# Second layernorm's rows turned on VectorE in 32 by 32 blocks instead of on TensorE, and the adapters' first product taken from the last GEMM's own operands

## The chip, the cores and the metric

The kernel runs on one core of a Trainium2 chip, in one launch. The metric is the device time of a whole execution in microseconds (us). Five engines run side by side, each with its own queue of instructions in a fixed order: TensorE (PE in the profile, with its weight loads as PEld), VectorE (DVE), ScalarE (ACT), GpSimd (POOL), and SyncE (SP), which here does nothing but issue the transfers between DRAM and on-chip memory (SBUF). They meet through semaphores only.

## The reference, cut to what matters

Eight sequences of 512 rows with 1024 columns, all in float32, go through an attention layer and a feed-forward layer. Both layers are set between two layernorms without scale or shift:

```python
x = x + layernorm(attention(layernorm(x)))      # 16 heads of 64, rotary, causal
x = x + layernorm(ffn(layernorm(x)))

def ffn(x):                                     # x: (8, 512, 1024)
    y = x @ weight.T + bias                     # 1024 x 1024
    A, Bw = lora_A[adapter_of_batch], lora_B[adapter_of_batch]   # rank 16, three adapters
    return y + use_lora * ((x @ A.T) @ Bw.T)    # per batch
```

The part that the change touches lies between `layernorm(x)` of the second line and the two products that read it. Both contract over the 1024 columns. TensorE contracts over the partitions of SBUF (128 of them), so the normalised rows, which are made with a row in each partition, must be turned: columns to the partitions, rows to the free axis.

## The kernel before

**Passes and ticks.** The last stage of the kernel is a loop over 16 passes, `q` = 0 to 15 (`products`, called at the end). Pass `q` below 8 multiplies the attention output of batch `q` with the output projection; pass `q` of 8 and above multiplies the normalised rows of batch `q - 8` with the feed-forward weight. Each pass is a 512 x 1024 x 1024 product done by two nested Strassen-like schemes of seven products each. That makes 49 small products, and each is one *tick*: two matmuls of 128 x 128 (stationary) by 128 x 256 (moving). `Group` holds seven ticks, in the order `SLOTS`; the groups come in the order `ORDER`. The stationary operand is a slot of `RX[q, n]` (the row side: `R11`, `R21`, `R12`, `R22` and the sums `T1` to `T4`, each tile with seven slots of 2 x 128 values); the moving one is a slot of the weights.

**What sets the order.** The order is written out by hand: `at(tick, fn)` hangs work on a tick, and `run(tick, ...)` emits, for each tick, first the extra TensorE work (`"pe"`), then the tick's product and the draining of the tick before, then everything else. So all engines' queues are interleaved by tick, and a queue may run ahead or behind only as far as its semaphores allow. Pass `q` starts at tick `49 q`.

**The accumulators.** A group adds its products in PSUM tiles `a` (one buffer), `b` (two), `c` (two) and `d` (one). `drain` empties them: ScalarE copies `a`, VectorE does the additions from `b`, `c` and `d` (line 337). `combine` (line 355) adds whole quarters on VectorE and GpSimd.

**The rows.** `plan_rows(q, base)` hangs the layernorms of pass `q`'s result on ticks that reach into pass `q + 1`: for row tile `t` (128 rows, four per batch), `k = base + 55 + 7 t`. There are statistics on VectorE, the normalisation on ScalarE (line 415), the residual sum on GpSimd (`add_row`, line 1107), the store of the sum (line 1112), then, for `q` below 8, statistics and normalisation again. The normalised rows land in the tile `row`. At `k + 20` and `k + 21` (ticks 26, 27 of the next pass for tile 0, then 33, 34, then 40, 41, then 47, 48) `transpose_x1` turns half a row tile each: four TensorE transposes into a PSUM tile `ptf` (line 1121), which ScalarE copies to `xT` (`keep_x1`, line 1125). `xT` has one buffer, for two row tiles. When two row tiles are turned, `lora_in` (line 1131) multiplies them with the adapters' A (eight matmuls, 64 x 256 each), `lora_keep` (line 1139, VectorE) masks the result to the batch's adapter, and `store_x1` stores it (`ht`, line 1144) and the turned rows (`x1t`, line 1145) to DRAM.

**The reading back.** In the passes from 7 on, `plan_right` loads the next pass's `R11`, `R21`, `R12`, `R22` at ticks 10, 17, 24 and 31 (`load_right`, line 255: four slots of raw rows in one transfer), and four ticks later GpSimd makes the other three slots and overwrites slot 2 with a difference (`sub_right`, line 263, the four steps of `SUM_R`). The sums `T1` to `T4` follow (line 275). `load_ht` (line 1084) reads `ht` back at tick 3 of the pass that uses it, and `sub_ht` (lines 1088 and 1089, GpSimd) makes its differences one tick later; the adapters' second product (line 322) uses them from tick 11 on.

**The loads' releasers.** A load of `R..` can only be issued when the last product that read its buffer is done; in the trace SP waits for that product at each of the four loads. All transfers go through SP's one queue. In both programs' instruction lists each transfer also waits for the transfer eight places before it in that queue: eight semaphores are used in turn.

Of the kernel before, what the change touches and what calls it, by code (L numbers as in the profile page):

```python
# [10 lines left out]
F32 = mybir.dt.float32  # L11
I32 = mybir.dt.int32
AF = mybir.ActivationFunctionType
ALU = mybir.AluOpType
# [16 lines left out]
ALL = slice(None)  # L31
# [101 lines left out]
def sandwich_kernel(  # L133
# [15 lines left out]
    nc = tc.nc  # L149
# [16 lines left out]
    x1t = [dram.tile([P, NT, NK, P], F32, name=f"x1t_{b}") for b in range(B)]  # L166
    htd = [dram.tile([P, S], F32, name=f"ht_{b}") for b in range(B)]


    vd = [dram.tile([P, NT, E], F32, name=f"vd_{b}") for b in range(B)]  # L170
# [23 lines left out]
    def at(tick, fn, kind=None):  # L194
        events[tick].append((kind, fn) if kind else fn)
# [14 lines left out]
    RX = {}  # L210
    C = {}
    hts = {}
# [34 lines left out]
    def load_right(pool, q, n):  # L247

        g, h = int(n[1]) - 1, int(n[2]) - 1
        open_right(pool, q, n)  # L250
        if q < B:
            nc.sync.dma_start(out=RX[q, n], in_=attn[q][:, g, h])
            return
        src = x1t[q - B]
        nc.sync.dma_start(
            out=RX[q, n][:, 0:4].rearrange("p (t k) c n -> p t (k c n)", t=2),
            in_=src[:, 2 * h : 2 * h + 2, ts(g, NH), :].rearrange("p t k n -> p t (k n)"),
        )

    def sub_right(q, n, eng):  # L260
        t = RX[q, n]
        for out, x, y in SUM_R:
# [21 lines left out]
    def open_c(q, tag):  # L284
# [3 lines left out]
            [P, 2, HALF], F32, tag=tag, bufs=1 + two, name=f"{tag}_{q}"  # L288
        )

    class Group:


# [7 lines left out]
        def product(self, p):  # L301
            l, r, a = SUBS[p]
            first = a not in self.acc
            if first:
                self.acc[a] = env["acc"].tile(
                    [P, SUB], F32, tag=a, bufs=ACCS[a], name=f"acc{a}_{self.name}"
                )
            acc = self.acc[a]
            left, right = self.W[self.L], RX[self.q, self.R]
            for k in range(2):  # L310
                if self.q < 0:
                    moving = left[:, SLOT_L[l], k, :]
                else:
                    moving = left[:, 4 * k : 4 * k + 4, SLOT_L[l], :]
                nc.tensor.matmul(  # L315
                    acc, lhsT=right[:, SLOT_R[r], k, :], rhs=moving,
                    start=(first and k == 0), stop=True, skip_group_check=True,
                )
            if self.lora and p in LORA_SUB:
                half, cols = self.lora  # L320
                i, c = LORA_SUB[p]
                nc.tensor.matmul(  # L322
                    acc, lhsT=hts[self.q - B][:, cols[c], :],
                    rhs=env["lb"][:, half * HALF + i * SUB : half * HALF + (i + 1) * SUB],
                    start=False, stop=True, skip_group_check=True,
                )
# [210 lines left out]
    for b in range(B):  # L537
        base = b * N2
# [514 lines left out]
    with ExitStack() as a:  # L1053
# [22 lines left out]
        at(N2 + 30, load_adapters)  # L1076

        NQ = 2 * B
        hto = {}

        def load_ht(b):

            t = hts[b] = lc.tile([P, 9, P], F32, tag="htb", name=f"htb_{b}")
            nc.sync.dma_start(out=t[:, 0:4], in_=htd[b][:, :].rearrange("p (t n) -> p t n", t=NT))

        def sub_ht(b):
            t = hts[b]
            nc.gpsimd.tensor_tensor(t[:, 4:6], t[:, 0:2], t[:, 2:4], op=ALU.subtract)
            nc.gpsimd.tensor_tensor(t[:, 6:9], t[:, 0:6:2], t[:, 1:6:2], op=ALU.subtract)  # L1089
# [23 lines left out]

        xT = {}

        def transpose_x1(q, t, g):
            if (q, t // 2) not in xT:
                xT[q, t // 2] = cp.tile([P, 2, NK, P], F32, tag="xT", name=f"xT_{q}_{t // 2}")
            pt = ps_t.tile([P, NH, P], F32, tag="tp", name=f"ptf_{q}_{t}_{g}")
            for k in range(NH):  # L1120
                nc.tensor.transpose(pt[:, k, :], row[q, t][:, ts(NH * g + k, P)], ident)
            return pt

        def keep_x1(q, t, g, pt):
            nc.scalar.copy(xT[q, t // 2][:, t % 2, ts(g, NH), :], pt)

        def lora_in(q, h):
            ph = ps_t.tile([P, NH, P], F32, tag="tp", name=f"ph_{q}_{h}")
            for k in range(NK):
                r = (k % 2) * HD  # L1130
                nc.tensor.matmul(  # L1131
                    ph[r : r + HD, 0:2, :], lhsT=la_sb[:, k, :], rhs=xT[q, h][:, :, k, :],
                    start=(k < 2), stop=(k >= NK - 2),
                )
            return ph

        def lora_keep(q, h, ph):
            ht = hto[q, h] = lc.tile([P, 2 * P], F32, tag="ht", name=f"ht_{q}_{h}")
            nc.vector.tensor_scalar(
                ht, ph[:, 0:2, :], sel[:, q : q + 1], idx_sb[:, 1:2], op0=ALU.mult, op1=ALU.add  # L1140
            )

        def store_x1(q, h):
            nc.sync.dma_start(out=htd[q][:, h * 2 * P : (h + 1) * 2 * P], in_=hto[q, h])
            nc.sync.dma_start(out=x1t[q][:, 2 * h : 2 * h + 2], in_=xT[q, h])

        def plan_right(q, base):

            if q > 1:
                at(base + 6, next_roles)  # L1150
            for n, k in (("R11", 10), ("R21", 17), ("R12", 24), ("R22", 31)):
                if q == 1 and n != "R22":
                    continue
                at(base + k, lambda n=n: load_right(gp, q, n))
                if q >= B:
                    at(base + k + 4, lambda n=n: sub_right(q, n, nc.gpsimd))
            for n, k in (("T1", 40 if q == 1 else 38), ("T2", 45), ("T4", 52), ("T3", 63)):
# [14 lines left out]
        def plan_rows(q, base):  # L1172

            for t in range(NT):
                k = base + 55 + 7 * t
                key = f"{'o' if q < B else 'y'}{q}_{t}"
                at(k + 2, lambda t=t: load_row(q, t))
                for m in range(4):
                    at(k + m, lambda t=t, m=m, key=key: stats(key, halves(q, t), m))
                for h in range(2):  # L1180
                    at(k + 4 + h, lambda t=t, h=h, key=key: norm(key, halves(q, t)[h], halves(q, t)[h]))
                    at(k + 6 + h, lambda t=t, h=h: add_row(q, t, h))
                at(k + 12, lambda t=t: store_rows(q, t))
                if q < B:
                    key = f"x{q}_{t}"
                    for m in range(4):
                        at(k + 12 + m, lambda t=t, m=m, key=key: stats(key, halves(q, t), m))
                    for h in range(2):
                        at(k + 16 + h, lambda t=t, h=h, key=key: norm(
                            key, row[q, t][:, ts(h, HALF)], halves(q, t)[h]  # L1190
                        ))
                    for g in range(2):
                        at(k + 20 + g, lambda t=t, g=g: transpose_x1(q, t, g), "pe")
                        at(k + 20 + g, lambda pt, t=t, g=g: keep_x1(q, t, g, pt), "post")
                    if t % 2:
                        at(k + 23, lambda t=t: lora_in(q, t // 2), "pe")
                        at(k + 23, lambda ph, t=t: lora_keep(q, t // 2, ph), "post")
                        at(k + 26, lambda t=t: store_x1(q, t // 2))

        def plan_last(q, base):  # L1200

# [159 lines left out]
```

## Time and profile before

| | us |
|---|---|
| median of 3 runs | 2499.29 (2498.07 to 2499.87) |
| span of the profiled execution | 2491.9 |
| what the median has around that span | 7.4 |
| the stage with the 16 passes: pass 1 starts at | 1703.57 |
| pass 7, 8, 9, 10 start at | 2007.28, 2062.78, 2119.65, 2171.19 |
| pass 15 starts at | 2425.44 |

The profile is of one execution on the chip; its own time is known by its span, from the first to the last instruction. A pass's start is the start of its first product in the TensorE timeline. In the last 16 passes the profile is to be read pass by pass: the passes below 8, those from 9 on, and the two at the seam (7 and 8, in which the feed-forward weights are loaded) are bound differently. Durations are of single instructions; a matmul's duration is longer than its pace, since matmuls are pipelined, so a pace is read from the starts of neighbours.

### The profile page before, as it was taken

Reading aid. Unit: us, or ns where it says so; the run is one execution under the profiler, and the core shown is the slowest. Engines: PE = TensorE matmul, PEld = TensorE weight load, DVE = VectorE, ACT = ScalarE, POOL = GpSimd, SP = SyncE. Lnnn points to the kernel's source line nnn. Section 1 sums busy time; section 2 is a strip of 40 time slices with the busy share of each in tenths; the row PEclk is TensorE's granted clock in tenths of the full one; section 3 lists DMA queues with packets and bytes.
Section 4 is the critical chain, followed back from the end, with each engine's and each line's share of the span. In section 5 each row is a group of like instructions: output and inputs, shape, how many; then the busy total and the mean of one; then the engine's idle time right before and its main releaser. Section 6 shows DMA issues by size and latency. Waiting matters only on the chain. (4 is left out here: it accounts for less than half of the span.)

```text
span 2491.9 us, 37087 instructions
## 1 busy us (share of the span) xinstructions
PE 2394.2 (96%) x12192; PEld 1880.4 (75%) x12192; DVE 1744.9 (70%) x3849; ACT 1094.4 (44%) x2749; POOL 1490.5 (60%) x1119
## 2 busy tenths in 40 slices
PE   6999999999999999999999999899999999999997
PEld 4787887877677777777777776458888878888886
DVE  8777767475857759486775957766777777766676
ACT  3323331026555556555555565763444544222222
POOL 3878875215263454637465363426777687888885
PEclk8999999999999999999999999899999999999999
DMA  7697787999899898988989895657566676434334
GB/s 261 198 299 251 241 272 235 344 307 285 238 302 285 258 328 255 328 267 297 326 264 346 250 327 174 219 182 266 178 202 212 217 278 240 137 126 153 132 106 140
DMA packets 415665, 606.00 MB, mean 243 GB/s; under 512 B 127889, under 2 KB 243601, under 8 KB 410866
## 3 DMA queue, kind: packets, MB, share of 16 engines
q1 hardware_dynamic: 415474, 603.64, 73.9%
q8 instruction: 98, 1.61, 0.3%
q14 instruction: 93, 0.76, 0.1%
HBM read 368.65 MB, written 201.33 MB: 229 GB/s over the span
## 5 line engine op out<-in xcount | busy, mean ns | idle before, releaser
L778 ACT ACTIVATE pr<-pr,nm 128x128 f32<-128x128 f32 (+3 forms) x512 | 280.9, 550 | 169.7 <-DVE nm L768 169.6
L792 ACT ACTIVATE pr<-pr,rs 128x128 f32<-128x128 f32 (+2 forms) x500 | 245.2, 549 | 119.9 <-DVE rs L786 119.8
L768 DVE CUSTOM_DVE_ANT_0 pr<-s,mask 128x128 f32<-128x128 f32 (+3 forms) x512 | 224.1, 484 | 41.8 <-PE s L747 39.7
L636 PE MATMUL acca_q_P<-xs,ls 128*128 128x256 f32 x896 | 217.3, 385 | 0.8 <-issue 0.8
L636 PE MATMUL accc_q_P<-xs,ls 128*128 128x256 f32 x896 | 217.7, 386 | 0.0
L636 PE MATMUL accb_q_P<-xs,ls 128*128 128x256 f32 x896 | 216.3, 384 | 0.8 <-DVE u_q_P L116 0.8
L1107 POOL TENSOR_TENSOR c<-c,row 128x512 f32<-128x512 f32 x120 | 160.7, 1360 | 87.4 <-ACT c L415 80.3
L636 PEld LDWEIGHTS acca_q_P<-xs,ls 128*128 128x128 f32 x896 | 165.3, 190 | 49.9 <-issue 19.1
L636 PEld LDWEIGHTS accc_q_P<-xs,ls 128*128 128x128 f32 x896 | 165.8, 190 | 48.4 <-issue 23.2
L636 PEld LDWEIGHTS accb_q_P<-xs,ls 128*128 128x128 f32 x896 | 165.4, 190 | 44.9 <-issue 6.2
L275 POOL TENSOR_TENSOR T<-R,T 128x512 f32<-128x512 f32 (+1 forms) x96 | 174.1, 1840 | 41.4 <-DVE u_P L337 21.0
L747 PE MATMUL s<-qk 64*128 64x128 f32 (+3 forms) x1024 | 193.8, 474 | 5.1 <-DVE nm L768 4.7
L806 PE MATMUL ptp<-ident,pr 128*128 128x128 f32 x1280 | 178.7, 278 | 11.0 <-DVE nm L768 4.8
L806 PEld LDWEIGHTS ptp<-ident,pr 128*128 128x128 f32 x1280 | 147.7, 142 | 43.1 <-ACT pr L792 15.8
L827 PE MATMUL po<-pT,v 128*64 128x512 f32 (+3 forms) x1024 | 157.4, 446 | 9.7 <-ACT pT L821 9.7
L562 POOL TENSOR_TENSOR wc_g<-wc_g 128x256 f32<-128x256 f32 (+1 forms) x120 | 124.1, 1053 | 65.5 <-DMA wc_g<-in_wqk_dram 43.5
L678 POOL TENSOR_TENSOR B_q<-B_q,m 128x1024 f32<-128x1024 f32 x14 | 35.0, 2497 | 199.0 <-DVE B_q L675 199.0
L827 PEld LDWEIGHTS po<-pT,v 128*64 128x64 f32 x1024 | 72.4, 139 | 102.0 <-issue 66.5
L337 DVE TENSOR_TENSOR p_P<-accb_P,p_P 128x256 f32<-128x256 f32 x109 | 45.0, 413 | 102.4 <-PE accb_P L315 53.5
L636 PE MATMUL accd_q_P<-xs,ls 128*128 128x256 f32 x448 | 108.7, 385 | 0.0
L337 DVE TENSOR_TENSOR u_P<-accb_P,p_P 128x256 f32<-128x256 f32 x109 | 46.1, 423 | 89.1 <-ACT p_P L342 89.0
L747 PEld LDWEIGHTS s<-qk 64*128 64x128 f32 x1024 | 73.1, 187 | 46.2 <-issue 27.9
(1108 smaller groups left out, 5809.7 us busy)
## 6 DMA issues: line engine op xcount, KB each, us to landing
ls<-wqk SPq DMA_DIRECT2D x392, 256.0 KB, 4.9
xs<-xop SPq DMA_DIRECT2D x392, 256.0 KB, 5.2
R<-attn SPq DMA_DIRECT2D x32, 896.0 KB, 5.5
wqk<-wc_g SPq DMA_DIRECT2D x16, 1568.0 KB, 9.3
x<-in_x_dram SPq DMA_DIRECT2D x32, 512.0 KB, 9.5
v<-vd SPq DMA_DIRECT2D x64, 256.0 KB, 5.0
attn<-ops SPq DMA_DIRECT2D x16, 1024.0 KB, 7.8
row<-in_x_dram SPq DMA_DIRECT2D x32, 512.0 KB, 5.9
```

The source lines that it names most:

```text
L275: eng.tensor_tensor(RX[q, n][:, c], RX[q, x][:, c], RX[q, y][:, c], op=ALU.subtract)
L337: add = lambda out, x, a: nc.vector.tensor_tensor(out, acc[a], x, op=ALU.add)
L562: eng.tensor_tensor(out, x, y, op=op)
L636: nc.tensor.matmul(acc[:, :, w, :], lhsT=ls[:, k, w, :], rhs=xs_[:, :, k, :], start=(first and w == 0 and k == 0), stop=True, skip_group_c ...
L678: eng.tensor_tensor(v, v, m[step - 4, q], op=ALU.add)
L747: nc.tensor.matmul(ps[:, j, at : at + L], lhsT=qT[r, qb], rhs=kT[r, : qb + 1], start=True, stop=True,)
L768: nc.vector.tensor_tensor_reduce(out=v[:, j, :], in0=self.ps[qb][:, j, :], in1=work2["mask"][:, S - L :], scale=-1.0 / HD**0.5, scalar=3.0e38,
L778: nc.scalar.activation(v[:, j, :], v[:, j, :], AF.Exp, bias=nm[:, j : j + 1], scale=-1.0, accum_out=sm[:, j : j + 1],)
L792: nc.scalar.mul(v, v, rs[:, j : j + 1])
L806: nc.tensor.transpose(pt[:, n, :], self.pr[qb][:, j, ts(kb, P)], ident)
L827: nc.tensor.matmul(po[j * HD : (j + 1) * HD, kb * P :], lhsT=self.v[:, kb, ts(j, HD)], rhs=self.pT[j][:, kb, kb * P :], start=(kb == 0), s ...
L1107: nc.gpsimd.tensor_tensor(c, c, row[q, t][:, ts(h, HALF)], op=ALU.add)
```

## The change

The normalised rows are no longer turned by TensorE. `turn_x1` issues one VectorE instruction per half row tile (128 x 512): it turns each block of 32 x 32 within itself and writes the blocks, with the values of two 128-column groups next to each other, to `xT` (now two buffers of half a row tile). The blocks reach their partitions by the transfers: `store_x1` issues four stores per half row tile, one for each group of 32 partitions, in runs of 512 B; `load_right` loads each operand in four transfers with runs of 256 B. The operand's raw slots now hold two columns groups interleaved, so that the matmuls read every second value (`by_blocks`).

The adapters' first product is no longer made from `xT`, but from the loaded operands: `lora_in` runs at ticks 22 and 35 of the passes 7 to 14, for the pass that follows, and reads the raw slots 0 to 3. The fourth step of `sub_right`, which overwrites slot 2, therefore moves behind it (ticks 22 and 35). `lora_keep` writes the result straight into the tile `htb`; its way through DRAM (`ht`) is gone, and `sub_ht` moves to tick 41 of the pass before.

```diff
-        src = x1t[q - B]
-        nc.sync.dma_start(
-            out=RX[q, n][:, 0:4].rearrange("p (t k) c n -> p t (k c n)", t=2),
-            in_=src[:, 2 * h : 2 * h + 2, ts(g, NH), :].rearrange("p t k n -> p t (k n)"),
-        )
+        for m in range(4):
+            t, k = divmod(m, 2)
+            nc.sync.dma_start(
+                out=RX[q, n][:, m].rearrange("p c n -> p (c n)").rearrange("p (a m) -> p a m", a=4),
+                in_=x1t[q - B][:, 2 * h + t, :, 2 * g + k, :],
+            )
...
+    def by_blocks(v, k):
+        return v.rearrange("p c n -> p (c n)").rearrange("p (n c) -> p n c", c=2)[:, :, k]
...
+                stays = right[:, k, :] if self.q < B else by_blocks(right, k)
                 nc.tensor.matmul(
-                    acc, lhsT=right[:, SLOT_R[r], k, :], rhs=moving,
+                    acc, lhsT=stays, rhs=moving,
...
-        def transpose_x1(q, t, g):
-            pt = ps_t.tile([P, NH, P], F32, tag="tp", name=f"ptf_{q}_{t}_{g}")
-            for k in range(NH):
-                nc.tensor.transpose(pt[:, k, :], row[q, t][:, ts(NH * g + k, P)], ident)
-        def keep_x1(q, t, g, pt):
-            nc.scalar.copy(xT[q, t // 2][:, t % 2, ts(g, NH), :], pt)
+        def turn_x1(q, t, g):
+            v = xT[q, t, g] = cp.tile([P, 4, 2, 32, 2], F32, tag="xT", bufs=2, name=f"xT_{q}_{t}_{g}")
+            nc.vector.transpose(
+                v[:, :, :, :, :].rearrange("p a k n c -> p k c a n"),
+                row[q, t][:, ts(g, HALF)].rearrange("p (k c a n) -> p k c a n", k=2, c=2, a=4),
+            )
+        def store_x1(q, t, g):
+            for a in range(4):
+                nc.sync.dma_start(
+                    out=x1t[q][:, t, a, ts(g, 2)].rearrange("(c e) k n -> e c (k n)", e=32),
+                    in_=xT[q, t, g][32 * a : 32 * a + 32].rearrange("e c k n m -> e c (k n m)"),
+                )
...
+                right = RX[b + B, f"R{k // NH + 1}{h + 1}"]
+                moving = right[:, k // 2 % 2 : 4 : 2].rearrange("p t c n -> p t (c n)").rearrange(
+                    "p t (n c) -> p t n c", c=2
+                )[:, :, :, k % 2]
                 nc.tensor.matmul(
-                    ph[r : r + HD, 0:2, :], lhsT=la_sb[:, k, :], rhs=xT[q, h][:, :, k, :],
+                    ph[r : r + HD, 0:2, :], lhsT=la_sb[:, k, :], rhs=moving,
...
-                    at(base + k + 4, lambda n=n: sub_right(q, n, nc.gpsimd))
+                    at(base + k + 4, lambda n=n: sub_right(q, n, nc.gpsimd, slice(0, 3)))
+            if q >= B:
+                for h, k in ((0, 22), (1, 35)):
+                    at(base + k, lambda h=h: lora_in(q - B, h), "pe")
+                    at(base + k, lambda ph, h=h: lora_keep(q - B, h, ph), "post")
+                    for g in range(2):
+                        at(base + k, lambda n=f"R{g + 1}{h + 1}": sub_right(q, n, nc.gpsimd, slice(3, 4)))
+                at(base + 41, lambda: sub_ht(q - B))
...
                     for g in range(2):
-                        at(k + 20 + g, lambda t=t, g=g: transpose_x1(q, t, g), "pe")
-                        at(k + 20 + g, lambda pt, t=t, g=g: keep_x1(q, t, g, pt), "post")
-                    if t % 2:
-                        at(k + 23, lambda t=t: lora_in(q, t // 2), "pe")
-                        at(k + 23, lambda ph, t=t: lora_keep(q, t // 2, ph), "post")
-                        at(k + 26, lambda t=t: store_x1(q, t // 2))
+                        at(k + 20 + g, lambda t=t, g=g: turn_x1(q, t, g))
+                        at(k + 22 + g, lambda t=t, g=g: store_x1(q, t, g))
...
-            if q >= B - 1 and q + 1 < NQ:
-                k = 10 if q == B - 1 else 52
-                at(base + k, lambda q=q: load_ht(q + 1 - B))
-                at(base + k + (6 if q == B - 1 else 1), lambda q=q: sub_ht(q + 1 - B))
```

More of the change, by code (lines that the diff above doesn't have):

```diff
@@ L165, in sandwich_kernel @@
     x1d = [dram.tile([P, NT, E], F32, name=f"x1_{b}") for b in range(B)]
-    x1t = [dram.tile([P, NT, NK, P], F32, name=f"x1t_{b}") for b in range(B)]
-    htd = [dram.tile([P, S], F32, name=f"ht_{b}") for b in range(B)]
+    x1t = [dram.tile([P, NT, 4, NH, 64], F32, name=f"x1t_{b}") for b in range(B)]
     vd = [dram.tile([P, NT, E], F32, name=f"vd_{b}") for b in range(B)]
@@ L253, in load_right, with sub_right @@
             return
-        src = x1t[q - B]
-        nc.sync.dma_start(
-            out=RX[q, n][:, 0:4].rearrange("p (t k) c n -> p t (k c n)", t=2),
-            in_=src[:, 2 * h : 2 * h + 2, ts(g, NH), :].rearrange("p t k n -> p t (k n)"),
-        )
-    def sub_right(q, n, eng):
+        for m in range(4):
[4 more added lines that the diff above has]
+            )
+    def sub_right(q, n, eng, steps=ALL):
         t = RX[q, n]
-        for out, x, y in SUM_R:
+        for out, x, y in SUM_R[steps]:
             eng.tensor_tensor(t[:, out], t[:, x], t[:, y], op=ALU.subtract)
@@ L308, in product @@
             acc = self.acc[a]
-            left, right = self.W[self.L], RX[self.q, self.R]
+            left, right = self.W[self.L], RX[self.q, self.R][:, SLOT_R[r]]
             for k in range(2):
+                stays = right[:, k, :] if self.q < B else by_blocks(right, k)
                 if self.q < 0:
@@ L1078, in sandwich_kernel @@
         NQ = 2 * B
[L1079 to L1084, printed above, removed]
         def sub_ht(b):
@@ L1114, in sandwich_kernel, with lora_in @@
         xT = {}
-        def transpose_x1(q, t, g):
-            if (q, t // 2) not in xT:
-                xT[q, t // 2] = cp.tile([P, 2, NK, P], F32, tag="xT", name=f"xT_{q}_{t // 2}")
-            pt = ps_t.tile([P, NH, P], F32, tag="tp", name=f"ptf_{q}_{t}_{g}")
-            for k in range(NH):
-                nc.tensor.transpose(pt[:, k, :], row[q, t][:, ts(NH * g + k, P)], ident)
-            return pt
-        def keep_x1(q, t, g, pt):
-            nc.scalar.copy(xT[q, t // 2][:, t % 2, ts(g, NH), :], pt)
-        def lora_in(q, h):
-            ph = ps_t.tile([P, NH, P], F32, tag="tp", name=f"ph_{q}_{h}")
+        def turn_x1(q, t, g):
[10 more added lines that the diff above has]
+                )
+        def lora_in(b, h):
+            ph = ps_t.tile([P, NH, P], F32, tag="tp", name=f"ph_{b}_{h}")
             for k in range(NK):
                 r = (k % 2) * HD
+                right = RX[b + B, f"R{k // NH + 1}{h + 1}"]
+                moving = right[:, k // 2 % 2 : 4 : 2].rearrange("p t c n -> p t (c n)").rearrange(
+                    "p t (n c) -> p t n c", c=2
+                )[:, :, :, k % 2]
                 nc.tensor.matmul(
-                    ph[r : r + HD, 0:2, :], lhsT=la_sb[:, k, :], rhs=xT[q, h][:, :, k, :],
+                    ph[r : r + HD, 0:2, :], lhsT=la_sb[:, k, :], rhs=moving,
                     start=(k < 2), stop=(k >= NK - 2),
@@ L1135, in lora_in, with lora_keep @@
             return ph
-        def lora_keep(q, h, ph):
-            ht = hto[q, h] = lc.tile([P, 2 * P], F32, tag="ht", name=f"ht_{q}_{h}")
+        def lora_keep(b, h, ph):
+            if not h:
+                hts[b] = lc.tile([P, 9, P], F32, tag="htb", bufs=2, name=f"htb_{b}")
             nc.vector.tensor_scalar(
-                ht, ph[:, 0:2, :], sel[:, q : q + 1], idx_sb[:, 1:2], op0=ALU.mult, op1=ALU.add
-            )
-        def store_x1(q, h):
-            nc.sync.dma_start(out=htd[q][:, h * 2 * P : (h + 1) * 2 * P], in_=hto[q, h])
-            nc.sync.dma_start(out=x1t[q][:, 2 * h : 2 * h + 2], in_=xT[q, h])
+                hts[b][:, 2 * h : 2 * h + 2], ph[:, 0:2, :], sel[:, b : b + 1], idx_sb[:, 1:2],
+                op0=ALU.mult, op1=ALU.add,
+            )
         def plan_right(q, base):
```

## The prediction

> **What bounds the kernel now.** I read the page's engine line first, then the busy time by pass, then the TensorE timeline where rows are turned, then the waits and the transfers.
>
> ```profile
> PE 2394.2 (96%) x12192; PEld 1880.4 (75%) x12192; DVE 1744.9 (70%) x3849; ACT 1094.4 (44%) x2749; POOL 1490.5 (60%) x1119
> ```
>
> TensorE is the bound on average. By pass (columns: stretch and length, busy time and instructions of PE, weight load, DVE, ACT, POOL, granted clock, DMA share, GB/s), for pass 3, pass 7, pass 11, and then two stretches of pass 3, ticks 21 to 36 and 37 to 48:
>
> ```profile
> 1804.11:1854.81 50.70, 50.23 (x262) 42.23 (x261) 37.11 (x83) 23.09 (x46) 36.80 (x25) 1.00 0.61 202
> 2007.28:2062.78 55.50, 52.35 (x261) 43.21 (x260) 39.30 (x86) 22.94 (x46) 47.17 (x40) 0.97 0.81 294
> 2222.12:2272.96 50.84, 49.58 (x229) 43.15 (x228) 34.75 (x68) 12.13 (x26) 41.58 (x37) 1.00 0.41 130
> 1821.50:1838.50 17.00, 16.53 (x85) 14.25 (x84) 14.64 (x38) 11.58 (x22) 9.81 (x7) 1.00 0.88 268
> 1838.50:1853.20 14.70, 14.70 (x82) 12.11 (x81) 8.11 (x19) 6.58 (x14) 9.54 (x8) 1.00 0.45 172
> ```
>
> Passes 1 to 6 have no slack on TensorE but 13.6 us on VectorE; VectorE is, however, nearly full in ticks 21 to 36 (14.64 of 17.0). Its light stretch comes after. The TensorE timeline (start, duration) around tick 40 of pass 3:
>
> ```profile
> 1836.28 0.60 PE L1121 MATMUL ptf<-ident,row 128*128 128x128 f32 x4
> 1836.72 1.03 PE L315 MATMUL accb_P<-wo_S,R 128*128 128x256 f32 x4
> 1837.59 0.60 PE L1121 MATMUL ptf<-ident,row 128*128 128x128 f32 x4
> 1838.02 1.03 PE L315 MATMUL acca_P<-wo_S,R 128*128 128x256 f32 x4
> 1838.89 1.03 PE L315 MATMUL accb_P<-wo_S,T 128*128 128x256 f32 x4
> 1839.85 1.95 PE L1131 MATMUL ph<-xT,la_sb 128*64 128x256 f32 x16
> ```
>
> Read the starts: four transposes hold TensorE for 1836.72 − 1836.28 = 0.44 us, a tick for 0.865 us, the adapters' eight matmuls for 1.9 us. A pass of 49 ticks alone is 42.4; pass 3 has 8 x 0.44 = 3.5 of transposes, 2 x 1.9 of adapters, and about 1 more.
>
> Two waits stand in the part changed: five times in passes 10 to 14 TensorE waits for the adapters' differences, once in pass 7 ScalarE waits for a store to free the turned rows:
>
> ```profile
> PE accd_P L322 <- POOL htb L1089: 6.2, 5, 1.3
> ACT xT L1125 <- DMA x1t<-xT: 5.9, 1, 5.9
> ```
>
> **The change part by part.** The sum is made on the profiled span, 2491.9; the median lies 7.4 above it, which I keep.
>
> *Transposes leave TensorE.* 64 groups x 0.436 us, in passes 1 to 8: −27.9. The 64 ScalarE copies (0.586 us each) go too, worth nothing: ScalarE is busy 23 of 50.7.
>
> *The adapters' first product moves.* Sixteen groups of 1.9 us leave passes 1 to 9 and come back in passes 7 to 14: net 0. Pass 1 loses 1.9, passes 2 to 6 lose 3.8 each, pass 9 gains 1.9, 10 to 14 gain 3.8 each.
>
> *The differences' wait.* They are made at tick 41 of the pass before, half a pass ahead of their use, without the trip through DRAM. Five waits of 1.24 with a restart of about 0.1 each: −6.7. POOL's work on them is only moved; what queues behind it there are the sums T2 and T4, needed in the next pass.
>
> Hidden everywhere, this is −34.7, or 2464.6.
>
> *VectorE's 64 turns.* The trace has no such instruction. Two copies and statistics of that size stand in it:
>
> ```profile
> L395 DVE BATCH_NORM_STATS2 bn_x<-c 128x6 f32<-128x512 f32 x64 | 41.8, 681 | 1.0 <-POOL c L1107 1.0
> ```
>
> I take T = 0.68 us, the nearest row: same 128x512, one input. Ends: 0.42 (what a 128x256 operation takes here, as if two values went per cycle) and 1.36 (two cycles for each). Eight a pass are 5.4, less two masks of 0.54: VectorE goes from 37.1 to 41.4 in a pass that would be 50.7 − 3.5 − 3.8 = 43.4. It still fits over the pass. It does not in the full stretch: there four turns make 14.64 + 4 x 0.68 = 17.36, while TensorE without its four groups of transposes needs 17.0 − 1.74 = 15.26. VectorE falls 2.1 us behind by tick 36.
>
> At ticks 40 and 41 it then meets its own stores. `xT` has two buffers, so turn three must wait for the stores of turn one. These are four transfers of 32 partitions each, and SP takes eight transfers in turn, each waiting for the one eight places before. Such waits show in the trace, and a 32-partition transfer costs SP 0.51 us to issue and 3.2 to land:
>
> ```profile
> SPq L621 <- DMA ls<-wqk: 19.3, 57, 1.2
> qk<-B_q SPq DMA_DIRECT2D x64, 128.0 KB, 3.2
> L687 SPq DMA_DIRECT2D qk<-B_q x64: 507/587/1498, 503.7 to 1567.5; - x64
> ```
>
> A turn at tick 33 is stored from 35 on, eight stores issue in 8 x 0.51 = 4.1 us, and the last lands 3.2 later: 7.3 us from tick 35, against 5 or 6 ticks (4.3 to 5.2 us) until the next turn. I charge 2.0 us of waiting on VectorE for that (ends 0, if POOL and ScalarE make it up, and 3). The turn stands in VectorE's queue ahead of the adds that drain accumulators `b`, `c`, `d`. The combines at ticks 45 to 52 add 2.0, the light stretch returns 0.8: VectorE is 2.1 + 2.0 + 2.0 − 0.8 = 5.3 late at worst. TensorE feels this beyond 3.0 us: `d` has one buffer, drained by three adds (1.25), and its next product comes five ticks (4.3) later. So 2.3 us in each of passes 1 to 6: +13.8 (ends: 0, and 4.3 each, 26).
>
> [...]
>
> *POOL in passes 1 to 6.* T1 to T4 of the next pass end 21.8 us after tick 38 and are needed 25 ticks (21.6) later, now by shorter passes. What TensorE gains here POOL may take back: pass 1, which has no transposes before it, shows 0.96 of such a wait. I count it inside the 2.3.
>
> *SP.* Passes 1 to 8 get 32 small stores for four large and lose the `ht` stores: +14 us of issue at 0.51. SP has room, but a store queued behind a load waits where the load waits for its buffer's last product (5.8 us at the longest in pass 3). Passes 7 to 14 get 16 loads for 4:
>
> ```profile
> R<-x1t SPq DMA_DIRECT2D x32, 512.0 KB, 4.4
> v<-vd SPq DMA_DIRECT2D x64, 256.0 KB, 5.0
> wqk<-wc_g SPq DMA_DIRECT2D x16, 1568.0 KB, 9.3
> wo_d<-wc_wo SPq DMA_DIRECT2D x8, 1568.0 KB, 7.3
> ```
>
> Runs of 512 B (`v`) cost little. Runs of 256 B (`wqk`) cost 9.3 where the same size in long runs took 7.3, a ratio of 1.27. Four issues add 3 x 0.37: R22 lands 4.4 to 6.1 us after tick 31's issue, I take 5.1 (4.4 is the row, and part of the fourth issue's 1.1 and of the 1.27 lies beside the others' landing).
>
> *The adapters' product wants R22 at tick 35.* From the issue to it TensorE has four ticks and three adapter matmuls of 0.43, 4.75 us. So 5.1 − 4.75 = 0.4 in each of passes 9 to 14: +2.4 (ends 0 and 1.4 each, 8). For R21 at tick 22 it has 5.6: nothing. Behind this wait stand TensorE's own ticks, so it is paid in full. POOL's fourth difference moves behind these matmuls; slot 2 is next read in the next pass, which covers it.
>
> *Pass 7* is 4.8 us longer than its neighbours: the store of the turned rows is late behind the new weights, ScalarE waits 5.9 for `xT`, its `U` after that, TensorE 2.6 on it, and POOL is busy 47.2. Now VectorE would wait there instead of ScalarE, at the same stores behind the same loads. I leave the 4.8 (ends −4.8, and +5: the first loads must be down by tick 22). *Pass 8:* R21 behind the last weights, +1.5 (ends 0 and 4; loads of rows landed in up to 8.0 there).
>
> *Operands read at a stride of two values.* Free in my sum. At half rate a weight load, now paced at 0.109 us, would take 0.218 against a matmul's 0.216: +0.4 a pass, +3; the adapters' moving operand at half rate +1.9 x 16 = +30.
>
> Sum: −27.9 − 6.7 + 13.8 + 2.4 + 0 + 1.5 = −16.9; 2491.9 + 7.4 − 16.9 = **2482**.
>
> **The rivals.** (A) As summed, 2482, own range 2470 to 2494.
>
> (B) Nothing is late: the light stretch absorbs VectorE's lag, 2464.6. For it: VectorE has slack over the pass. Against: 14.64 of 17.0 where the turns fall.
>
> (C) Stores come late at every row tile, not only the third: SP's turn of eight ties them to loads in flight, and about 3 us more are lost in each of passes 1 to 6: +18, 2500, no change. For it: DMA share 0.88 in that stretch. Against: 6 us between tiles.
>
> (D) The other side: a turn takes 1.36, since it must write columns across partitions and interleave them. VectorE has 37.1 − 1.1 + 8 x 1.36 = 46.9 a pass, 48.9 with its wait, against 45.7 in my sum: +3.2 x 6, and 2.7 in each of passes 7 and 8: 2482 + 24.6 = 2507. Each 0.1 us of T beyond 0.68 costs some 3.5, so it decides from T = 1.17 on.
>
> (E) The moving operand at stride two goes at half rate: 2482 + 33 = 2515, slower. Nothing in the trace reads so. [...]
>
> **How the numbers follow.** A 0.38, B 0.12, C 0.16, D 0.16, E 0.13, something unlisted 0.05. A change of 0.2% (5 us) is about what measurement can tell. Faster: 0.36 of A, B, 0.03 of C: 0.51. Same: 0.02 of A, 0.08 of C, 0.03 of D: 0.13. Slower: the rest of C and D (0.05, 0.13), E, unlisted: 0.36. The range takes in B at its lower end and most of D at its upper, leaving the upper half of E and the unlisted: 2464 to 2514.
>
> **What will show it.** Passes 2 to 6 near 45.7 us (B: 43.4; D: 48.9). DVE rows for the turn: 0.68 each, the third tile's with a wait for `x1t<-xT` of about 2. TensorE waits on VectorE's drains, first `d`. In passes 9 to 14 no wait on `htb`, a short one of `ph` on `R<-x1t`, and eight matmuls still in 1.9; pass 11 near 50.84 + 3.8 − 1.35 + 0.4 = 53.7. I am wrong if T exceeds 1.0, if the group of eight takes more than 2.2, if stores hold VectorE at several tiles, or if pass 7 moves by more than 5.

## The result

The changed kernel takes 2519.06 us (2516.36 to 2523.42, 4 runs) against 2499.58 before: ratio 1.0076, 95% interval 1.0057 to 1.0095. That is 19.5 us slower, where 16.9 us faster was forecast; the time lies above the range too.

The page's engine line of the changed kernel, and its windows for passes 3, 7, 8 and 11 (columns as before):

```profile
PE 2381.0 (95%) x11936; PEld 1863.3 (74%) x11936; DVE 1773.1 (70%) x3913; ACT 1059.4 (42%) x2685; POOL 1495.1 (59%) x1119
```

```profile
1806.74:1854.93 48.19, 44.18 (x198) 36.65 (x197) 39.98 (x89) 18.63 (x38) 36.80 (x25) 1.00 0.71 208
2001.10:2061.72 60.62, 49.74 (x229) 39.31 (x228) 43.39 (x93) 18.98 (x38) 46.68 (x41) 0.94 0.83 231
2061.72:2126.63 64.91, 56.20 (x260) 46.58 (x259) 47.44 (x98) 18.98 (x38) 44.45 (x37) 0.97 0.84 242
2236.53:2290.15 53.62, 53.62 (x262) 46.41 (x260) 35.65 (x70) 12.14 (x26) 42.75 (x37) 1.00 0.42 118
```

TensorE lost work in the passes below 8 (its busy time in pass 3 fell from 50.23 to 44.18), but they did not shrink with it: 4 us of pass 3, 11 of pass 7 and 9 of pass 8 are now idle, where before there were 0.5, 3.2 and 0.2. In pass 11 TensorE is busy without a gap. Pass 8 of the kernel before, for comparison:

```profile
2062.78:2119.65 56.87, 56.71 (x291) 47.93 (x290) 42.70 (x92) 23.26 (x46) 42.80 (x35) 1.00 0.70 250
```

From the starts of the passes' first products, in us (one traced execution each):

| | before | forecast | changed |
|---|---|---|---|
| passes 1 to 6 | 303.7 | 275.7 | 294.5 |
| pass 7 | 55.5 | 52.0 | 60.6 |
| pass 8 | 56.9 | 54.9 | 64.9 |
| pass 9 | 51.5 | 53.8 | 56.0 |
| passes 10 to 14 | 254.3 | 268.5 | 268.5 |

The miss has two places: 18.8 us in passes 1 to 6, and 18.6 in passes 7 and 8. Another 2.2 lies in pass 9. (The trace of the changed kernel also starts pass 1 3.0 us later than the trace of before; e11 below settles that.)

**Passes 1 to 6.** The turn's own row, and the waits in the six passes (engine, line, waited for; total, times, longest):

```profile
L1118 DVE STREAM_TRANSPOSE xT<-row x64: 695/702/720, 1732.1 to 2130.1; 128x512 f32<-128x512 f32 x64
```

```profile
ACT sd_x L408 <- DVE mv_x L403: 51.2, 24, 5.5
...
DVE xT L1118 <- DMA x1t<-xT: 11.6, 6, 3.2
PE acca_P L320 <- ACT c L354: 10.4, 18, 1.0
PE acca_P L320 <- ACT U L354: 10.1, 6, 3.0
...
PE accc_P L320 <- DVE A L342: 4.8, 5, 1.0
...
PE accb_P L320 <- POOL T L275: 1.3, 1, 1.3
```

A turn takes 0.70 us, near the estimate of 0.68. VectorE's six waits for stores (11.6 us, the line `DVE xT`) all stand before the first turn of the third row tile, one in each pass, 1.9 us on the mean. TensorE waits 20.5 us for ScalarE's copies of accumulator `a`, and never for `d`. ScalarE is idle more than half the time (busy 18.6 of 48.2 us in pass 3); what makes its copies late is the first line, 24 waits of the square root `sd_x` for VectorE's statistics `mv_x` (six waits with 12.2 us before). The order on VectorE shows why. Its timeline in pass 3 around the last row tile (start, duration), then ScalarE's and TensorE's:

```profile
1845.53 0.68 DVE L400 BATCH_NORM_STATS2 bn_x<-c 128x6 f32<-128x512 f32 x1
1847.41 0.71 DVE L1118 STREAM_TRANSPOSE xT<-row 128x512 f32<-128x512 f32 x1 [1.20 <-DMA x1t<-xT]
1848.05 0.65 DVE L400 BATCH_NORM_STATS2 bn_x<-c 128x6 f32<-128x512 f32 x1
1848.73 0.21 DVE L403 BATCH_NORM_AGGREGATE mv_x<-bn_x 128x2 f32<-128x12 f32 x1
```

```profile
1849.04 0.29 ACT L408 ACTIVATE sd_x<-mv_x,eps 128x1 f32<-128x1 f32 x1 [3.49 <-DVE mv_x L403]
1849.24 0.35 ACT L354 COPY U<-acca_P 128x256 f32<-128x256 f32 x1
```

```profile
1849.64 1.13 PE L320 MATMUL acca_P<-wo_S,R 128*128 128x256 f32 x4 [0.94 <-ACT U L354]
```

The turn, with its wait for a store, stands between the two halves of the next row tile's statistics. The square root waits for both halves, and behind it in ScalarE's queue stands the copy that empties `a`. There is one buffer of `a`, so TensorE waits for that.

**Passes 7 and 8.** TensorE's waits there, then TensorE's timeline around the adapters' product of the second row half in pass 7, and the queue of SP:

```profile
PE ph L1138 <- DMA R<-x1t: 13.7, 4, 5.8
```

```profile
2037.56 1.13 PE L1138 MATMUL ph<-R,la_sb 128*64 128x256 f32 x8
2044.51 1.97 PE L1138 MATMUL ph<-R,la_sb 128*64 128x256 f32 x8 [5.83 <-DMA R<-x1t]
2046.41 1.79 PE L320 MATMUL accb_P<-wo_S,T 128*128 128x256 f32 x4
2048.04 1.03 PE L320 MATMUL acca_P<-wo_S,T 128*128 128x256 f32 x4
```

```profile
2028.16 4.02 SPq L255 DMA_DIRECT2D R<-x1t  x4
2032.28 2.03 SPq L1111 DMA_DIRECT2D x<-c  x2
2034.40 4.16 SPq L1125 DMA_DIRECT2D x1t<-xT  x8
2038.66 0.39 SPq L1102 DMA_DIRECT2D row<-in_x_dram  x1
2039.16 2.05 SPq L255 DMA_DIRECT2D R<-x1t  x4
```

The half on R12 runs at 2037.6, then TensorE stands 5.8 us until R22 is there. R22's four loads are issued from 2039.16 on, after the product's turn has already come: in SP's single queue they stand behind eight stores of turned rows, 4.16 us. These in turn stand behind R12's loads, which SP could issue only at 2028.16, when TensorE, which had stood 2.21 us for R21, had done the last product on R12's buffer.

### The profile page after: what moved, and what is told of

It reads as the page before. It is cut to its first block, busy times and chain, and to the rows that moved or that the text cites. A ratio compares the mean times of both kernels' runs of the same rounds, so it can differ in the third digit from the quotient of the medians.

```text
span 2516.8 us, 37015 instructions
## 1 busy us (share of the span) xinstructions
PE 2381.0 (95%) x11936; PEld 1863.3 (74%) x11936; DVE 1773.1 (70%) x3913; ACT 1059.4 (42%) x2685; POOL 1495.1 (59%) x1119
## 4 chain that ended last, share of the span: by engine, by line
PE 58%; DVE 7%; DMA 7%; POOL 4%; issue 3%; ACT 3%; SPq 1%; DVEq 0%; ACTq 0%; POOLq 0%
PE acca_q_P L641 7%; PE accc_q_P L641 7%; PE accb_q_P L641 7%; PE s L752 6%; PE po L832 5%; PE ptp L811 5%; PE accb_P L320 4%; PE accc_P L320 4%; PE acca_P L320 4%; PE accd_q_P L641 3%; PE accd_P L320 2%; DMA x1t<-xT 1%; POOL c L1106 1%; PE ph L1138 1%; DMA attn<-opt 1%
## 5 line engine op out<-in xcount | busy, mean ns | idle before, releaser
L811 PE MATMUL ptp<-ident,pr 128*128 128x128 f32 x1280 | 179.1, 278 | 13.8 <-ACT pr L797 6.2
L263 POOL TENSOR_TENSOR R<-R 128x256 f32<-128x256 f32 x128 | 96.5, 764 | 18.2 <-DMA R<-x1t 11.2
L826 DVE COPY pT<-ptp 128x384 f32<-128x384 f32 (+1 forms) x129 | 78.7, 614 | 39.0 <-PE ptp L811 39.0
```

The lines of the kernel that those rows point to most:

```text
L811: nc.tensor.transpose(pt[:, n, :], self.pr[qb][:, j, ts(kb, P)], ident)
```

## The experiments

All ratios are to the kernel before; the changed kernel's is 1.0076. A difference between lengths of passes is from one trace each: passes 1 to 6, which e1 and e6 leave as they are in the changed kernel, took 294.5, 295.5 and 298.0 in those three traces, so some 3.5 us there mean nothing.

**e1, the adapters' product later.** It is cut in two (`g` is 0 for the four matmuls on R1x, 1 for those on R2x), each with its fourth difference.

```diff
-                for h, k in ((0, 22), (1, 35)):
+                for h, g, k in ((0, 0, 30), (0, 1, 31), (1, 0, 36), (1, 1, 43)):
...
-                at(base + 41, lambda: sub_ht(q - B))
+                at(base + 48, lambda: sub_ht(q - B))
```

> The adapters' first product is made later: for the first row half in two steps at ticks 30 and 31 in place of 22, for the second at ticks 36 (R12) and 43 (R22) in place of 35; the differences at tick 48. In the changed kernel TensorE waits before these products about 2.6 and 7.1 us in pass 7, 2.3 and 5.4 in pass 8, 1 in pass 9, 18 in all. Theory (the loads are late and the product asks too early): 15 to 18 us go, near 2502. Rival (the transfers are so late that the sums T1 and T2 and the next pass wait in the product's place): less than 6 us go, 2513 or more. The passes 1 to 6 stay at 48.7 us by both.

Measured: 2521.53 us, ratio 1.0095 (1.0070 to 1.0120): nothing gained. The waits of `ph` for loads are gone, yet passes 7 and 8 took 65.0 and 60.3, together 125.4 (125.5 in the changed kernel). The product in four parts also has a price where nothing is late: passes 10 to 14 took 54.25 each, 0.6 more. The waits in passes 7 and 8:

```profile
ACT sd_x L408 <- DVE mv_x L403: 36.5, 8, 10.4
...
DVE xT L1118 <- DMA x1t<-xT: 11.9, 3, 6.3
...
PE acca_P L320 <- ACT U L354: 9.2, 2, 5.6
PE acca_P L320 <- ACT c L354: 5.6, 3, 4.2
```

My theory fell: that the product asks too early is not the only bound. Behind its wait lay another on the same jam of transfers: VectorE's turn waits for stores (6.3 at the longest), and through the statistics ScalarE and TensorE wait with it. The named rival had other details (the sums T1 and T2), but its number was right.

**e2, one store for each half row tile; e3, four stores for each whole row tile.**

```diff
-            for a in range(4):
-                nc.sync.dma_start(
-                    out=x1t[q][:, t, a, ts(g, 2)].rearrange("(c e) k n -> e c (k n)", e=32),
-                    in_=xT[q, t, g][32 * a : 32 * a + 32].rearrange("e c k n m -> e c (k n m)"),
+            nc.sync.dma_start(
+                out=x1t[q][:, t, :, ts(g, 2)].rearrange("p a k n -> p a (k n)"),
+                in_=xT[q, t, g].rearrange("p c k n m -> p c (k n m)"),
```

> One store of 128 partitions for each turned half row tile in place of four of 32 partitions, same bytes and same runs of 512 B; the blocks then lie at the wrong places in DRAM, so the placing is left out of the computation. Theory (SP's half microsecond for each issue is what makes stores and the loads behind them late): VectorE's waits for the stores (15.7 us in nine places) go, R22 is issued some 3 us earlier in passes 7 and 8; 12 to 18 us in all, near 2503. Rival (the transfers' own time, or the turn itself, is the cause): less than 5 us go.

> The turned rows lie in one buffer of a whole row tile, and four stores of 32 partitions in runs of 1 KB take it away (16 stores a pass in place of 32). By the theory of the issues about half of what one store for each half tile gives: 6 to 9 us, near 2511; a new wait is possible, since one buffer must be stored before the next tile's first turn. By the rival 0, or slower by that wait.

Measured: e2 2507.68 us, ratio 1.0041 (1.0027 to 1.0054); 0.35% or 9 us of the loss are the stores' splitting, a little less than the theory said. Passes 1 to 6 took 288.5, 6.0 less; VectorE's waits for stores went from 15.7 to 11.0 us (in passes 1 to 6 from 11.6 to 5.3), not to nothing. Pass 8 lost 4.4 us, pass 7 only 0.7: there R22 was issued 8.6 us behind its tick 31 (at 2029.87, in a pass that started at 1994.46, 31 ticks counted at 0.865 and without waits), in the changed kernel 11.2, and the rest of the gain went into a longer wait for ScalarE's copy of `U` (3.5 us).

e3: 2524.23 us, ratio 1.0104 (1.0079 to 1.0129), so not the 6 to 9 us of gain: its intervals touch the changed kernel's. With one buffer VectorE's waits for stores rose to 15.4 us in passes 1 to 6 (11.6), and those passes took 303.2. The run does not tell the price of an issue apart from that of the buffer.

**e4, the turning back on TensorE.** Row tiles are transposed and copied as before the change, in half tiles; one store each, one load for each operand; only the adapters' product is moved as in the change.

```diff
+            xT[q, t, g] = cp.tile([P, NH, P], F32, tag="xT", bufs=2, name=f"xT_{q}_{t}_{g}")
+            nc.scalar.copy(xT[q, t, g], pt)
...
+            nc.sync.dma_start(out=x1t[q][:, t, ts(g, NH)], in_=xT[q, t, g])
...
-                        at(k + 20 + g, lambda t=t, g=g: turn_x1(q, t, g))
+                        at(k + 20 + g, lambda t=t, g=g: transpose_x1(q, t, g), "pe")
+                        at(k + 20 + g, lambda pt, t=t, g=g: keep_x1(q, t, g, pt), "post")
```

> The turning goes back to TensorE and ScalarE, with the old order of the rows in DRAM, one store for each half row tile and one load for each operand; the adapters' first product stays at ticks 22 and 35 on the loaded operands. If VectorE's turns and their many transfers are what costs: passes 2 to 6 at 50.7 - 3.8 = 47.0 (48.7 in the changed kernel), the waits of the adapters' product in passes 7 and 8 a third of 17 us, in all some 20 us less than the changed kernel, near 2497. If the loads are late behind the new weights whatever turns the rows, these waits stay, and it ends near 2510.

Measured: 2493.97 us, ratio 0.9985 (0.9973 to 0.9997). Passes 2 to 6 took 47.05 each (47.0 expected), passes 7 and 8 53.0 and 58.9:

```profile
1807.56:1854.59 47.03, 46.08 (x229) 40.28 (x228) 36.43 (x81) 23.32 (x46) 36.74 (x25) 1.00 0.64 213
1995.73:2048.69 52.96, 50.59 (x262) 42.05 (x261) 40.77 (x86) 23.47 (x46) 46.45 (x40) 1.00 0.83 289
```

So the whole loss is in the turns and their transfers; the rest of the change, the adapters' product from the operands and the differences without DRAM, is a small gain with the old turning. Pass 3 with 3.5 us more on TensorE is 1.2 us shorter than in the changed kernel.

**e5, the turns at other ticks.**

```diff
-                        at(k + 20 + g, lambda t=t, g=g: turn_x1(q, t, g))
-                        at(k + 22 + g, lambda t=t, g=g: store_x1(q, t, g))
+                        at(k + 20 + g + (0, 4, 3, 3)[t], lambda t=t, g=g: turn_x1(q, t, g))
+                        at(k + 22 + g + (0, 4, 3, 3)[t], lambda t=t, g=g: store_x1(q, t, g))
```

> The turns of row tiles 1, 2 and 3 (and their stores) 4, 3 and 3 ticks later: out of the stretch in which VectorE makes the two halves of the next row tile's statistics, whose square root stands on ScalarE ahead of the copies that empty accumulator a. Theory (a turn of 0.70 between the two halves holds ScalarE, and so TensorE): the stalls at ticks 35 and 42 of passes 1 to 6 (0.5 and 1 to 3 us) go, 2 us a pass, 12 to 18 us in all, near 2504. Rival (VectorE is simply overfull, or waits for the stores wherever the turns stand): less than 4 us.

(The ticks of the stalls are one too low there by the code's count: they are 36 and 43. So is that of the stall in e10: it is tick 2.) Measured: 2513.80 us, ratio 1.0057 (1.0042 to 1.0072): 0.19%, 5 us of the 12 to 18 expected. Passes 1 to 6 fell by 7.0 to 287.5, and the waits that the theory names fell, here in the six passes:

```profile
ACT sd_x L408 <- DVE mv_x L403: 38.0, 24, 3.1
DVE xT L1118 <- DMA x1t<-xT: 12.3, 10, 2.3
...
PE acca_P L320 <- ACT c L354: 6.2, 11, 1.3
PE acca_P L320 <- ACT A L354: 5.7, 4, 2.8
```

The waits for ScalarE's copy of `U` (10.1) are gone; new ones for the copy of `A` at the end of the pass (5.7) took half of it. Passes 7 and 8 grew by 3.7 us. The intervals of the two whole times touch, so that the place of the turns counts rests on these waits and on passes 1 to 6, which fall by 7.0 here and by 6.8 from e7 to e8 below. In the whole time it is a third of what I gave it.

**e6, one load for each operand; e7, one store and one load; e8, these and the moved turns.**

```diff
-        for m in range(4):
-            t, k = divmod(m, 2)
-            nc.sync.dma_start(
-                out=RX[q, n][:, m].rearrange("p c n -> p (c n)").rearrange("p (a m) -> p a m", a=4),
-                in_=x1t[q - B][:, 2 * h + t, :, 2 * g + k, :],
-            )
+        nc.sync.dma_start(
+            out=RX[q, n][:, 0:4].rearrange("p (t a) c n -> p t a (c n)", t=2)[:, :, :, 0:256],
+            in_=x1t[q - B][:, 2 * h : 2 * h + 2].rearrange("p t a k n -> p t (a k n)")[
+                :, :, 512 * g : 512 * g + 512].rearrange("p t (a m) -> p t a m", m=256),
+        )
```

> One load of each operand in long runs in place of four in runs of 256 B, same bytes; the values then lie at the wrong places in the operands, so the placing is left out of the computation. Stores and turns as in the changed kernel. Theory (the four-part loads are half of the jam in passes 7 and 8): passes 7 to 9 shorter by 6 to 10 us, passes 1 to 6 as they were, near 2511. Rival (the jam comes from the stores and turns alone): less than 3 us.

> One store for each half row tile and one load for each operand, both without the placing: what is left of the change is the turns on VectorE at their places and the adapters' product on the operands. Passes 2 to 6 as with one store alone (47.1 mean), passes 7 and 8 near those of the kernel with TensorE's turns (53.0 and 58.9) if the transfers make the jam, in all near 2497; if VectorE's turns themselves wait or hold ScalarE there, passes 7 and 8 stay near 60 and it ends near 2506.

> As the run with one store and one load, and the turns of row tiles 1 to 3 moved 4, 3 and 3 ticks later. If the turn's place between the halves of the statistics is what is left of the loss, passes 2 to 6 go from 47.1 to 44 to 45 us and the whole ends 12 to 18 us under that run, near 2482, which is what was forecast; if VectorE is overfull, no more than 4 us are gained.

(The 47.1 that two of these give for passes 2 to 6 with one store is the median of the five; their mean is 47.6.)

| | us | ratio (95%) | passes 1 to 6 | pass 7 | pass 8 |
|---|---|---|---|---|---|
| changed | 2519.06 | 1.0076 (1.0057 to 1.0095) | 294.5 | 60.6 | 64.9 |
| e2, one store | 2507.68 | 1.0041 (1.0027 to 1.0054) | 288.5 | 60.0 | 60.5 |
| e6, one load | 2511.37 | 1.0046 (1.0031 to 1.0061) | 298.0 | 57.0 | 59.7 |
| e7, both | 2499.05 | 1.0000 (0.9986 to 1.0014) | 288.6 | 55.7 | 58.4 |
| e8, both, turns moved | 2493.48 | 0.9989 (0.9979 to 0.9999) | 281.8 | 55.0 | 59.5 |
| e4, TensorE's turns | 2493.97 | 0.9985 (0.9973 to 0.9997) | 287.3 | 53.0 | 58.9 |

Each of the two splittings costs 0.30 to 0.35%; with both gone the whole loss is gone, and the sum of the two alone (0.65%) is near the two together (0.76%). Loads act on passes 7 and 8 (8.9 us), stores on passes 1 to 6 (6.0) and 7 and 8 (5.1). R22's issue begins 38.1 us into pass 7 in the changed kernel, 34.6 in e6 (where the eight stores alone hold SP for 6.05) and 31.0 in the kernel before; from there to its last landing it takes 6.1, 5.2 and 5.3 us. So most of what R22 gains in e6 is the issue. e6 also has longer runs of bytes, and no run divides the rest. But e7 also shows that the turns on VectorE, at no cost for the placing, gain nothing over the kernel before, and e8 only 0.11%, where I expected 12 to 18 us under e7.

**e9 and e10, less work on GpSimd, or on VectorE.** Both start from e8; the diff is e9's, and e10 has (48, 52) in the place of (38, 47).

```diff
-                if base + k >= AHEAD:
+                if base + k >= AHEAD and not (1 <= q <= 6 and k in (38, 47)):
```

> The kernel with one store, one load and moved turns, without GpSimd's two additions of whole quarters (c21) in passes 1 to 6, which are left out of the computation: 6 us less on GpSimd a pass, of 36.8, all of it in the chain of sums from tick 38 to the next pass's tick 14. If GpSimd's chain is what keeps passes 2 to 6 at 47.0 us where the ticks alone are 42.4, they fall to 44 to 45.5, 9 to 15 us in all; if VectorE keeps them there, they stay within 0.7 us.

> The kernel with one store, one load and moved turns, without VectorE's additions of whole quarters at ticks 48 and 52 (c12 and c22) in passes 1 to 6, which are left out of the computation: 3.3 us less on VectorE a pass, of 40. If VectorE keeps passes 2 to 6 at 47.0 us, they fall by 1.5 to 3 us (the stall at tick 1, 1.2 to 1.7 us, goes), 9 to 18 us in all; if GpSimd does, they stay within 0.7 us.

Measured: e9 2488.98 us, ratio 0.9964 (0.9951 to 0.9977); passes 1 to 6 279.8, 2.0 less than e8; passes 2 to 6 fell from 47.2 to 46.9 on the mean. e10 2488.28, ratio 0.9961 (0.9946 to 0.9976); passes 1 to 6 276.3, 5.5 less, passes 2 to 6 46.3. Neither is what was expected of a single bound. In passes 1 to 6, e9 has 30.8 us less of GpSimd's busy time than e8 (191.2 for 222.0) and the same of VectorE's; e10 has 18.0 less of VectorE's (222.1 for 240.1), but also 10.3 less of GpSimd's, whose additions got shorter. The whole times are alike, and the 3.5 us between the two in passes 1 to 6 are what two traces of the same code differ by, so the runs do not say which engine counts for more. The stall that e10 was to remove stayed: TensorE waits five times for VectorE's `A`, 6.0 us in all, in e8 and in e10.

**e11, the kernel before once more.**

> The kernel before, unchanged, for a second trace. In the traces of the changed kernel and all its variants pass 1 starts at 1706.6 to 1710.8, in the one trace of before at 1703.6, though nothing ahead of it differs in the instructions. If that is spread between executions, this trace starts pass 1 up to 3 us later than the first; if the changed kernel's stage ahead is really slower, it starts within 1 us of 1703.6.

Measured: ratio 1.0003 (0.9994 to 1.0013). Its second trace starts pass 1 at 1709.49, not at 1703.57. So the 3.0 us ahead of pass 1 are spread between executions and no work of the change.

**e12, a version that beats both.** e4 with the adapters' product at ticks 25 and 37.

```diff
-                for h, k in ((0, 22), (1, 35)):
+                for h, k in ((0, 25), (1, 37)):
```

> The kernel with TensorE's turns, whole stores and whole loads, and the adapters' product three and two ticks later (25 and 37). Its waits for the loads in passes 7 and 8 come to 4.9 us there; if nothing takes their place, 2 to 4 us less than that kernel, 0.997 to 0.998 of the kernel before. If the wait moves on, as with the later product of the changed kernel, 0.9985 as it was.

Measured: 2488.42 us, ratio 0.9969 (0.9955 to 0.9982), 0.3% under the kernel before. Passes 7, 8 and 9 came to 52.5, 56.7 and 53.6 (53.0, 58.9 and 54.0 in e4). In these two traces asking later gains 3.1 us in the three passes; the intervals of the whole times touch. That it helps here and not in e1 fits the cause found there, since here no turn on VectorE waits for stores, but no run shows that this is the reason.

## Why the prediction was wrong

- **The plain counts were right.** Transposes, adapters' groups and the differences' wait: passes 10 to 14, where only these and the 0.4 for R22 act, were forecast at 268.5 and took 268.5. No wait on `htb` is left in them. That they agree to the tenth is chance: TensorE never waits for R22 there, so the 2.0 for it was not paid; about 1 for the stride (next point) and 1 that no run divides stand in its place. A turn was taken at 0.68 and measured 0.70, so rival D is out. VectorE's wait for its stores was charged at 2.0 a pass, at the third row tile, and took 1.9 there.
- **Operands at a stride of two values are all but free**, as summed; rival E is out. In the changed kernel a matmul of the adapters' group takes 387 ns and a weight load of a pass from 8 on 196; in e4, with contiguous operands, 379 and 190. Passes 10 to 14 are 0.2 us longer each than in e4. That the time came close to E's 2515 is chance.
- **"TensorE feels this beyond 3.0 us": this step failed in passes 1 to 6.** I sized VectorE's lag at 5.3 and let accumulator `d` forgive 3.0. The lag reached TensorE on another way, through the statistics, ScalarE's square root and the copies of `a` behind it: the square root's waits went from 12.2 to 51.2 us, TensorE's for `a` from 2.6 to 20.5, and it never waited for `d`. The 13.8 became 32.6. By the runs, 6.0 of the 18.8 missed is the splitting of the stores (e2) and 6.8 the turns' place between the statistics (e7 to e8; 7.0 from the changed kernel to e5), each from single traces. The last 6 us were not taken apart. In the changed kernel's trace stand, beside the copies of `a`, 4.8 us of waits for VectorE's `A` and about 1.8 at half clock (last section).
- **"I leave the 4.8" and "R21 behind the last weights, +1.5": these steps failed in passes 7 and 8.** I priced each transfer's landing by itself, and not the queue it is issued from. 32 stores and 16 loads of about half a microsecond each in one queue, in each of two passes whose transfers had DMA at 0.81 and 0.70 before (0.83 and 0.84 now), put R22's issue behind its use. 8.9 us of the 18.6 go with whole loads (e6), 5.1 with whole stores (e2), 11.4 with both (e7), and 13.7 with TensorE's turns (e4). My end for pass 7 was +5; it was 8.6 above the forecast. What is left in e7 over the forecast, 7 us, is not split further.
- **Rival C's** +18 lies near the 18.8 missed in passes 1 to 6, but by chance: it had stores late at every row tile, and there VectorE waits for them at the third tile alone, as the sum had it. It did not count the way to TensorE either, nor passes 7 and 8 (in pass 7 the waits come at two tiles, 2.3 and 1.2 us). B, that nothing is late, was wrong; even e8, without the cost of the placing, is 29 us above it.
- **The stores' splitting**, e2's 9 us, is not explained by the time of the transfers themselves: a store of 64 KB from 32 partitions lands in 1.8 us (median), so the four of a half tile, issued 0.52 apart, end after 3 x 0.52 + 1.8 = 3.4; the single store of 256 KB in e2 lands in 3.2. What differs is the time that SP is held, 2.1 against 0.37. In the kernel before, 128 KB by 32 partitions (`qk`) land in 3.2 us and the 128 KB of `ht` by 128 partitions in 1.7, but in different stages and in other runs of bytes. No run holds the issues and varies the partitions, so whether their number counts is not shown.
- **A count.** The prediction has four large stores of turned rows a pass in the kernel before; its trace has 16 in eight passes, two a pass. Its +14 us of issue would be about 15.

## What to carry to other kernels

Work moved off the bounding engine is only gained if the queue that takes it lets it wait (here the square root's waits behind VectorE's turns went from 12.2 to 51.2 us in passes 1 to 6): look at what stands directly behind the new instruction, on its engine and on the engine that this one releases, before looking at busy shares. Splitting a transfer in four was priced here by the issuing queue (2.1 us of SP for four stores, 0.37 for one) and by what is queued behind it there; where a new consumer of a load is put earlier than the old one, check the load's issue and not its landing alone. When a wait is removed at a jam and nothing is gained, as in e1 (ratio 1.0095 after 1.0076), find the second wait on the same cause.

## What the runs showed of the hardware

A wait of TensorE can cost more than it lasts. After the wait of 2.97 us in pass 1 the next two ticks took 1.87 and 1.64 us in place of 0.865:

```profile
1750.79 2.07 PE L320 MATMUL acca_P<-wo_S,R 128*128 128x256 f32 x4 [2.97 <-ACT U L354]
1752.66 1.81 PE L320 MATMUL accc_P<-wo_S,T 128*128 128x256 f32 x4
1754.30 1.03 PE L320 MATMUL accc_P<-wo_S,R 128*128 128x256 f32 x4
```

The granted clock (the number after the last bracket) is half in these two ticks, and full after them:

```profile
1750.79:1752.66 1.87, 1.87 (x5) 1.51 (x6) 1.25 (x5) 0.50 (x1) 0.00 (x0) 0.51 0.52 108
1752.66:1754.30 1.64, 1.64 (x5) 1.34 (x4) 0.42 (x1) 1.32 (x3) 0.00 (x0) 0.52 0.27 51
1754.30:1756.00 1.70, 1.70 (x9) 1.51 (x8) 1.46 (x2) 0.00 (x0) 1.40 (x2) 1.00 0.53 103
```

The same follows the 5.83 above (granted clock 0.50 and 0.58 in the matmuls on R22 and the tick after them) and a wait of 4.00 us in pass 8 (0.60 and 0.50), and not the waits of 2.21 us in pass 7 (for R21), 2.27 in pass 4 and 2.42 in pass 8 (1.00 after each). So each of the three adds 1.7 to 1.8 us, and I had priced waits by their length and a restart of 0.1. The kernel before has one such case too: after its wait of 2.57 us in pass 7 two ticks took 1.87 and 1.55 (0.50 and 0.55), and the prediction's account of the 4.8 us of that pass leaves this out. The length alone does not decide: at the start of pass 2 TensorE waits 1.96 us for VectorE's `A` in e9 and 1.95 in e10; the next two ticks took 0.97 and 0.87 us in e9, 1.39 and 1.70 in e10. What decides it, no run shows.
